# Layer 1's self-attention in a two-layer decoder: layernorms in halves, later projections, earlier first shifts, and two small copies as maxima over one element

## The chip, the cores and the metric

The kernel runs on one core of one Trainium2 chip. The metric is the device time of one execution in microseconds (us), taken as the median of several runs; lower is better.

A core has a matrix engine (TensorE, PE in the profile; its weight loads are the row PEld), a vector engine (VectorE, DVE), an activation engine (ScalarE, ACT), a general engine (GpSimd, POOL) and a queue engine that issues DMAs (SyncE, SP). Matmuls write to PSUM, of which this kernel uses three banks for short products (the tile `bank`), two double banks (the tile `wide`) and one bank for sums (the tile `acc`) in the stage that is changed.

## The reference

The whole computation is two post-layernorm decoder layers over x of shape (2, 1024, 256) in fp32. What is changed here is the fourth of six blocks, layer 1's self-attention:

```python
def _L1_attn_ref(x, W_qkv, b_qkv, W_proj, b_proj):
    B, N, C = x.shape                      # 2, 1024, 256
    qkv = x @ W_qkv + b_qkv
    qkv = qkv.reshape(B, N, 3, 16, 16).transpose(2, 0, 3, 1, 4)
    q, k, v = qkv
    scores = einsum('bhqd,bhkd->bhqk', q, k) * 16 ** -0.5
    attn = softmax(scores)
    out = einsum('bhqk,bhkd->bhqd', attn, v)
    return out.transpose(0, 2, 1, 3).reshape(B, N, C) @ W_proj + b_proj
...
x = _layernorm(x + _L0_ffn_ref(x, ...))    # its end lies in the changed stage
x = _layernorm(x + _L1_attn_ref(x, ...))
x = _layernorm(x + _L1_xattn_ref(x, ctx_1024, ...))
```

## The kernel before

The 2048 tokens are four groups g of 512 tokens (two for each batch b), held as tiles of 128 tokens: `x[g]` is 128 x 4 x 256. The stage lies in `l1_attn`.

**Units and steps.** A step is one batch b, one quad of four heads and one half qb of the queries, so there are 16 steps in the order of `steps`. A step has eight units, one for each block `kt` of 128 keys, 128 units in all. A unit computes the scores of its keys against 512 queries for four heads (`products`, L1270), adds a shift to them by a second matmul (L1276), takes the exponential on ScalarE (L1282), and one unit later multiplies the result with the values (`mix`, L1296). The shift is the row maximum of the scores, negated; it has to be known before a step begins. So every unit also computes two pieces of the scores of a step ahead (`maxima`, L1225, 18 pieces in front) and VectorE reduces each half of them (L1235), out of the three banks.

**The shifts.** At the last unit of a step, `shifts(n)` takes the smaller of two halves (L1245), rounds it to the matmul format (a copy, L1247), copies that into the tile `cz` (L1248) and writes the rest beside it by a subtraction (L1249), all on VectorE and all on 128 x 16 elements. `shifted(n)` turns `cz` on TensorE (L1256), and VectorE evacuates it.

**The other work.** Everything else is laid out by hand in a table: `at(unit, f, ...)` puts a call at the end of a unit. TensorE, VectorE and ScalarE run in the order in which their instructions are written (`manual_schedule`); instructions of GpSimd and DMAs from SP are ordered by a planner and start when what they need is there. The calls are:
- `project` computes 512 columns of q or k for eight heads (L1134), ScalarE adds the bias (L1139), VectorE cuts it to its high part (L1142), GpSimd subtracts (L1143): a split. `stacks` copies the parts by DMA into the layout of the score matmuls (32 DMAs for two steps), and `values` computes the values of two blocks of keys.
- `taken` and `quotient` divide a finished step by its row sums.
- For each finished group: `turned` transposes the result, `output` multiplies with the output weights and adds x plus the bias (a residual sum on GpSimd, L1342), then takes the moments (L175, L176, L178 on VectorE, a power on GpSimd, L180); `normed` scales (L228), and `onward` transposes x for the next block.
- The same `weigh` (moments) and `normed` end the block before for groups 2 and 3, at units 11 to 13 and 19 to 21.

With `first = 8 * n` for step n, projections stand at `first - 26`, stacks at `first - 20`, values at `first - 22`. The first group that is finished here has `first` 48, the next 56, the third 112; the fourth is finished in the next block, through the list `ends`.

Ahead of unit 0 there are nine units that only compute maxima, out of the double banks (L1230), beside the first values and projections, and after them the first shifts.

The moments are written tile by tile:

```python
for k, i in enumerate(tiles):
    nc.vector.bn_stats(st, r[:, i, :])
    nc.vector.bn_aggr(mv[:, k, :], st)
nc.vector.tensor_scalar(ve[:, 0:n], mv[:, 0:n, 1], EPS, None, ALU.add)
nc.gpsimd.tensor_tensor(rstd[:, 0:n], ve[:, 0:n], self.nhalf[:, 0:n], ALU.pow)
```

A second helper, `weighed`, is there already for another block: it does two tiles at a call, both `bn_stats` before both `bn_aggr`, and the power at the second call. `scaled_half` scales two tiles.

Of the kernel before, what the change touches and what calls it, by code (L numbers as in the profile page):

```python
# [9 lines left out]
F32 = mybir.dt.float32  # L10
# [5 lines left out]
ALU = mybir.AluOpType  # L16
AX = mybir.AxisListType

P = 128
B, S, D = 2, 1024, 256  # L20
# [13 lines left out]
class Decoder:  # L34
# [1110 lines left out]
    def l1_attn(self):  # L1145
        nc, t = self.nc, self.t
        w, parts = self.l1w, self.l1parts
        wo = self.weight(t["L1_attn_W_proj"].rearrange("(c p) o -> p c o", p=P), 2, D)
        with ExitStack() as s:
# [5 lines left out]
            for k in range(2):  # L1155
                f = self.weight(None, 1, P)[:, 0, :]
# [10 lines left out]
            def project(b, m, name, blk):  # L1167
                self.l1_project(b, m, name, blk, self.xT[2 * b + blk])
# [41 lines left out]
            def maxima(u, early=False):  # L1210

                if u >= 16 * len(steps):
                    return
                n, k = u // 16, u % 16 // 8
                qt, kb = divmod(u % 8, 2)
                b, quad, qb = steps[n]
                jp = 2 * quad + k
                if u % 16 == 0:
                    most[n] = self.sm.tile([P, 2, 4, 4], F32, tag="most", name="most")
                q0 = qb * 512 + qt * P  # L1220
                both = self.wide() if early else None
                sc = [both[:, a, :] if early else self.bank() for a in range(2)]
                for a in range(2):
                    rows = slice(64 * a, 64 * a + 64)
                    nc.tensor.matmul(  # L1225
                        sc[a], lhsT=stack[b, jp, "q"][rows, q0 : q0 + P],
                        rhs=stack[b, jp, "k"][rows, kb * 512 : (kb + 1) * 512], start=True, stop=True,
                    )
                if early:
                    nc.vector.tensor_reduce(  # L1230
                        most[n][:, kb, qt, k : k + 3 : 2], both, AX.X, ALU.max, negate=True
                    )
                for a in range(0 if early else 2):
                    h = 2 * a + k
                    nc.vector.tensor_reduce(  # L1235
                        most[n][:, kb, qt, h : h + 1], sc[a], AX.X, ALU.max, negate=True
                    )

            def shifts(n):

                if n >= len(steps):
                    return
                cz = zeros[n % 2]
                nm = self.sm.tile([P, 4, 4], F32, tag="nm8", name="nm8")
                nc.vector.tensor_tensor(nm, most[n][:, 0], most[n][:, 1], ALU.min)  # L1245
                hi = self.sm.tile([P, 4, 4], F32R, tag="nmh", name="nmh")
                nc.vector.tensor_copy(hi, nm)  # L1247
                nc.vector.tensor_copy(cz[:, :, :, 0], hi.bitcast(F32))  # L1248
                nc.vector.tensor_tensor(cz[:, :, :, 1], nm, hi.bitcast(F32), ALU.subtract)  # L1249

            def shifted(n):
# [74 lines left out]
            aT, nxT = {}, [None] * NG  # L1326

            def turned(g):
                a_tok = tok[g // 2, g % 2]
                aT[g] = self.weight(None, 2, GT)  # L1330
                for c in range(2):
                    ps = self.bank()
                    for i in range(4):
                        nc.tensor.transpose(
                            ps[:, i * P : (i + 1) * P],
                            a_tok[:, i, 2 * c : 2 * c + 2, :].rearrange("p a i -> p (a i)"), self.ident,
                        )
                    self.evac(aT[g][:, c, :], ps)

            def output(g):  # L1340
                r = self.rp.tile([P, 4, D], F32, tag="r", name="r")
                nc.gpsimd.tensor_tensor(  # L1342
                    r, self.x[g], self.lbp.unsqueeze(1).to_broadcast([P, 4, D]), ALU.add
                )
                for i in range(0, 4, 2):
                    ps = self.bank().rearrange("p (i d) -> p i d", i=2)
                    for k in range(2):
                        for c in range(2):
                            nc.tensor.matmul(
                                ps[:, k, :], lhsT=aT[g][:, c, (i + k) * P : (i + k + 1) * P],  # L1350
                                rhs=wo[:, c, :], start=c == 0, stop=c == 1,
                            )
                    rv = r[:, i : i + 2, :]
                    nc.vector.tensor_tensor(rv, ps, rv, ALU.add)
                weigh(g, r)

            sums = {}

            def weigh(g, r=None):
                r = self.sums[g] if r is None else r  # L1360
                sums[g] = r, self.moments(r, range(4))

            def normed(g):
                r, moments = sums.pop(g)
                self.x[g] = self.xp.tile([P, 4, D], F32, tag="x", name="xg")
                self.scaled(self.x[g], r, range(4), *moments)

            def onward(g):
                nxT[g] = self.transposed(self.x[g])
# [4 lines left out]
            def at(unit, f, *args):  # L1374
                extra.setdefault(unit, []).append((f, args))

            for g, unit in ((2, 11), (3, 19)):
                for k, f in enumerate((weigh, normed, self.turned)):
                    at(unit + k, f, g)
            last = 8 * len(steps)  # L1380
            both = [(name, blk) for name in "qk" for blk in range(2)]
            for n, (b, quad, qb) in enumerate(steps):
                first = 8 * n
                if qb == 0:
                    for i, (name, blk) in enumerate(both):
                        if quad % 2 == 0 and n > 4:
                            at(first - 26 + i, project, b, quad // 2, name, blk)
                    for i, name in enumerate("qk" if n else ()):
                        for k in range(2):
                            at(first - 20 + 2 * k + i, stacks, b, 2 * quad + k, name)  # L1390
                    if quad == 0 and n:
                        for k in range(4):
                            at(first - 22 + k, values, b, k)
                at(first + 8, taken, n)
                at(first + 9, quotient, n)
                if quad == 3 and n < len(steps) - 1:
                    g = 2 * b + qb
                    for k, f in ((10, turned), (11, output), (13, normed), (15, onward)):
                        at(first + k, f, g)

            def others(unit):
                for f, args in extra.pop(unit, ()):
                    f(*args)

            engines = {mybir.EngineType.PE, mybir.EngineType.DVE, mybir.EngineType.Activation}
            with self.tc.manual_schedule(engines=engines):
                for k in range(2):
                    for name in "kq":
                        stacks(0, k, name)
                jobs = [lambda k=k: values(0, k) for k in range(4)]  # L1410
                jobs += [lambda a=a: project(0, 1, *a) for a in both]
                for unit in range(-9, 0):
                    maxima(2 * unit + 18, True)
                    maxima(2 * unit + 19, True)
                    if jobs:
                        jobs.pop(0)()
                    others(unit)
                shifts(0)
                shifted(0)
                late = None  # L1420
                for unit in range(last + 1):

                    n = (unit + 1) // 8 if unit % 8 == 7 else None
                    if n:
                        shifts(n)
                    maxima(2 * unit + 18)
                    now = products(*divmod(unit, 8)) if unit < last else None
                    maxima(2 * unit + 19)
                    if n:
                        shifted(n)  # L1430
                    if late:
                        mix(*late)
                    late = now
                    others(unit)
                for unit in sorted(extra):
                    others(unit)
            self.ends = [lambda f=f: f(3) for f in (turned, output, normed, onward)]
            self.xT = nxT


# [460 lines left out]
```

## Time and profile before

| | us |
|---|---|
| median of 3 runs | 2443.83 |
| lowest and highest of them | 2438.67, 2444.66 |
| the profiled execution: its time | 2446.0 |
| the profiled execution: its span | 2444.2 |

| engine | busy us | share of the span | instructions |
|---|---|---|---|
| TensorE, matmul | 2337.1 | 96% | 14037 |
| TensorE, weight load | 1592.3 | 65% | 14037 |
| VectorE | 1676.1 | 69% | 2920 |
| ScalarE | 1107.5 | 45% | 1726 |
| GpSimd | 913.5 | 37% | 751 |

The mean granted clock of TensorE is 0.977 of full speed. Unit 0 begins at 1784.7 us of the span and unit 127 ends near 2229.7. Matmuls are pipelined and their ends are modelled, so that TensorE looks busy where it is not at its peak: what counts is what an instruction waited for. In a row of a group, the numbers after the bar are the busy time, the mean length of one in ns, and the idle time of the engine in front of it with what ended that. In a row of waits, they are the time, how often, and the longest. In a row of the timeline there are the start, the length (of several, if x is over 1), the engine, the line, and in brackets the idle time before it and what released it.

### The profile page before, as it was taken

The numbers are of one execution on the slowest core, as the hardware profiler recorded it, in microseconds if no ns is written. First come the engines' busy times: TensorE is split into PE (matmuls) and PEld (weight loads), VectorE is DVE, ScalarE is ACT, GpSimd is POOL, SyncE is SP. The second block draws the span as 40 slices with busy tenths as digits, with TensorE's granted clock in tenths as the row PEclk, the third lists the DMA queues.
The fourth block names the chain that finished last, engine by engine and source line by source line (L and its number), as shares of the span: only waits on it lengthen the run. The fifth ranks groups of instructions, "written<-read, shape, count | busy, mean of one in ns | idle before, by whom it ended". The sixth has DMA issues, their size and how long they took to land.

```text
span 2444.2 us, 37232 instructions
## 1 busy us (share of the span) xinstructions
PE 2337.1 (96%) x14037; PEld 1592.3 (65%) x14037; DVE 1676.1 (69%) x2920; ACT 1107.5 (45%) x1726; POOL 913.5 (37%) x751
## 2 busy tenths in 40 slices
PE   7999999999998999999999999999999999999974
PEld 3445545545545668899999999999744444555742
DVE  6888888988785235555565555546789687995786
ACT  4665565565562322333233333333156454665344
POOL 4666576666565222433243342432310001002412
PEclk9999999999999999999999999999989999999996
DMA  7888788788787001001010010100212122210001
GB/s 158 171 169 165 151 171 166 143 172 165 151 171 180 1 1 42 18 22 30 10 36 29 18 47 1 48 1 1 55 20 45 25 36 34 43 28 1 1 1 35
DMA packets 275715, 168.81 MB, mean 69 GB/s; under 512 B 47584, under 2 KB 262224, under 8 KB 275536
## 3 DMA queue, kind: packets, MB, share of 16 engines
q1 hardware_dynamic: 239120, 148.07, 28.8%
q10 hardware_dynamic: 36416, 18.36, 3.7%
q8 instruction: 111, 1.82, 0.3%
q14 instruction: 68, 0.56, 0.1%
HBM read 34.23 MB, written 2.10 MB: 15 GB/s over the span
## 4 chain that ended last, share of the span: by engine, by line
PE 79%; DVE 10%; SPq 3%; issue 3%; DMA 3%; ACT 2%; POOL 1%; ACTq 0%; POOLq 0%; DVEq 0%
PE unit L965 16%; PE acc L1013 9%; PE wide L325 7%; PE bank L1013 7%; PE acc L407 6%; PE acc L1296 5%; PE bank L1225 3%; PE bank L280 3%; SPq L386 3%; DVE most L1235 2%; PE bank L705 2%; PE wide L692 2%; PE bank L425 2%; PE wide L1270 2%; PE wide L1276 2%
## 5 line engine op out<-in xcount | busy, mean ns | idle before, releaser
L340 DVE TENSOR_REDUCE nm<-wide 128x1 f32<-128x1024 f32 x256 | 300.8, 1213 | 56.1 <-PE wide L325 55.2
L1235 DVE TENSOR_REDUCE most<-bank 128x1 f32<-128x512 f32 x476 | 296.0, 682 | 24.8 <-PE bank L1225 24.0
L1282 ACT ACTIVATE w<-wide 128x1024 f32<-128x1024 f32 x256 | 248.2, 1022 | 141.9 <-PE wide L1276 131.8
L325 PE MATMUL wide<-k,q 64*128 64x512 f32 x1024 | 273.0, 627 | 17.7 <-ACT p L345 14.8
L356 POOL TENSOR_SCALAR p<-p,sums 128x1024 f32<-128x1024 f32 x128 | 143.5, 1121 | 265.8 <-DVE sums L353 265.8
L407 PE MATMUL acc<-turned,v 128*64 128x256 f32 x2048 | 236.5, 384 | 1.9 <-ACT aoT L74 1.0
L407 PEld LDWEIGHTS acc<-turned,v 128*64 128x64 f32 x2048 | 144.1, 137 | 114.3 <-issue 34.2
L954 ACT ACTIVATE mhT<-mhT,cols 128x256 f32<-128x256 f32 (+1 forms) x256 | 143.3, 607 | 144.2 <-DVE mhT L982 101.1
L345 ACT ACTIVATE p<-wide,nm 128x1024 f32<-128x1024 f32 x128 | 142.8, 1116 | 135.4 <-DVE nm L340 111.2
L370 DVE STREAM_TRANSPOSE blocks<-p 128x1024 f32<-128x1024 f32 x128 | 158.0, 1234 | 49.6 <-DMA q<-q 21.5
L863 POOL TENSOR_TENSOR hs<-hs,mhT 128x1024 f32<-128x1024 f32 x31 | 102.4, 3304 | 237.4 <-DVE hs L861 220.2
L325 PEld LDWEIGHTS wide<-k,q 64*128 64x128 f32 x1024 | 90.0, 186 | 143.3 <-issue 71.3
L965 PE MATMUL unit<-xT,w 128*128 128x256 f32 x768 | 182.0, 379 | 0.0
L1022 DVE SCALAR_TENSOR_TENSOR r<-acc,gates,r 128x128 f32<-128x128 f32 x256 | 77.7, 345 | 138.1 <-PE acc L1013 138.1
L180 POOL TENSOR_TENSOR rstd<-ve,nhalf 128x4 f32<-128x4 f32 (+2 forms) x24 | 22.0, 918 | 383.5 <-DVE ve L178 383.2
L370 DVE STREAM_TRANSPOSE blocks<-r 128x1024 f32<-128x1024 f32 x128 | 153.8, 1202 | 0.0
L1225 PE MATMUL bank<-kst,qst 64*128 64x512 f32 x476 | 139.2, 480 | 14.1 <-DVE most L1235 13.8
L965 PEld LDWEIGHTS unit<-xT,w 128*128 128x128 f32 x768 | 141.0, 190 | 17.1 <-issue 0.5
L1225 PEld LDWEIGHTS bank<-kst,qst 64*128 64x128 f32 x476 | 67.7, 189 | 127.7 <-DVE most L1235 105.2
L356 POOL TENSOR_SCALAR r<-r,sums 128x1024 f32<-128x1024 f32 x128 | 143.8, 1123 | 0.0
L345 ACT ACTIVATE r<-wide,nm 128x1024 f32<-128x1024 f32 x128 | 142.2, 1111 | 1.1 <-DVE nm L340 0.9
L1296 PE MATMUL acc<-w,v 128*32 128x512 f32 x1024 | 141.6, 626 | 0.0
(341 smaller groups left out, 4592.1 us busy)
## 6 DMA issues: line engine op xcount, KB each, us to landing
turned<-blocks SPq DMA_DIRECT2D x636, 128.0 KB, 2.8
turned<-blocks ACTq DMA_DIRECT2D x132, 128.0 KB, 3.0
w<-in_L_ffn_W SPq DMA_DIRECT2D x16, 1024.0 KB, 5.7
q<-q SPq DMA_DIRECT2D x64, 128.0 KB, 2.3
k<-k SPq DMA_DIRECT2D x32, 128.0 KB, 2.4
qst<-qh SPq DMA_DIRECT2D x48, 64.0 KB
qst<-ql SPq DMA_DIRECT2D x48, 64.0 KB, 2.4
kst<-kh SPq DMA_DIRECT2D x48, 64.0 KB
```

What stands on the lines that cost most here:

```text
L325: nc.tensor.matmul(sc[h][:, kb, :], lhsT=q[rows, qi, at : at + P], rhs=k[rows, ki, :], start=True, stop=True,)
L340: nc.vector.tensor_reduce(nm, sc, AX.XY, ALU.max, negate=True)
L345: nc.scalar.activation(p, sc.rearrange("p a c -> p (a c)"), AF.Exp, bias=nm, accum_out=sums[:, 0, h : h + 1],)
L356: nc.gpsimd.tensor_scalar(p, p, sums[:, 1, h : h + 1], 1.0, ALU.mult, ALU.mult)
L370: nc.vector.transpose(blocks[m][:, :, h, qt, :], p.rearrange("p (j q) -> p j q", q=32))
L407: nc.tensor.matmul(av[own[h], 0:256].rearrange("p (t i q) -> p i t q", t=2, i=4), lhsT=vals[u][:, kt, own[h]], rhs=p[:, h], start=kt == 0, ...
L965: nc.tensor.matmul(v[:, m, :], lhsT=up[e][k][:, f : f + P], rhs=self.halves[g][k], start=k in (1, 2, 5) and m == 0, stop=True, skip_group_ ...
L1013: nc.tensor.matmul(ps[at][:, m * P : (m + 1) * P], lhsT=h[k][:, c, m * P : (m + 1) * P], rhs=down[e][k][:, c, :], start=k in (1, 2, 5) and ...
L1225: nc.tensor.matmul(sc[a], lhsT=stack[b, jp, "q"][rows, q0 : q0 + P], rhs=stack[b, jp, "k"][rows, kb * 512 : (kb + 1) * 512], start=True, s ...
L1235: nc.vector.tensor_reduce(most[n][:, kb, qt, h : h + 1], sc[a], AX.X, ALU.max, negate=True)
L1282: nc.scalar.activation(slot[:, k, :], ps[k].rearrange("p a q -> p (a q)"), AF.Exp, scale=0.25)
L1296: nc.tensor.matmul(mixed[n][o : o + 32, :], lhsT=vals[b][:, kt, 17 * h : 17 * h + 32], rhs=pT[:, a, :], start=kt == 0, stop=kt == 7, tile_ ...
```

## The change

- A layernorm comes in pieces of two tiles: `weigh` and `normed` take a half, and each half has a unit of its own. The output is also split into halves, and the residual sum has a function of its own, `residual`. With groups 2 and 3 of the block before, moments go to units 11, 12 and 19, 20, scaling to 13, 14 and 21, 22, the turn to 15 and 23. For the groups that finish here, the output goes to `first` + 11 and 12, the moments to 13 and 14, the scaling to 15 and 16, the turn onward to 17. `weighed` and `scaled_half` take the place of `moments` and `scaled`.
- Projections, stacks and values stand three units later: `first - 23`, `first - 17`, `first - 19`.
- The first shifts are written ahead of the last two maxima of the nine early units.
- The two small copies of the shifts (L1247, L1248) become maxima over an axis of one element, which give the same values.

```diff
@@ shifts @@
-                nc.vector.tensor_copy(hi, nm)
-                nc.vector.tensor_copy(cz[:, :, :, 0], hi.bitcast(F32))
+
+                nc.vector.tensor_reduce(hi, nm.unsqueeze(3), AX.X, ALU.max)
+                nc.vector.tensor_reduce(
+                    cz[:, :, :, 0], hi.bitcast(F32).unsqueeze(3), AX.X, ALU.max
+                )
                 nc.vector.tensor_tensor(cz[:, :, :, 1], nm, hi.bitcast(F32), ALU.subtract)
@@ output, weigh, normed @@
-            def output(g):
-                r = self.rp.tile([P, 4, D], F32, tag="r", name="r")
+            def residual(g):
+                r = sums[g] = self.rp.tile([P, 4, D], F32, tag="r", name="r")
                 nc.gpsimd.tensor_tensor(
                     r, self.x[g], self.lbp.unsqueeze(1).to_broadcast([P, 4, D]), ALU.add
                 )
...
+            def output(g, half):
+                ps = self.bank().rearrange("p (i d) -> p i d", i=2)
...
+                rv = sums[g][:, 2 * half : 2 * half + 2, :]
+                nc.vector.tensor_tensor(rv, ps, rv, ALU.add)
...
-            def weigh(g, r=None):
-                r = self.sums[g] if r is None else r
-                sums[g] = r, self.moments(r, range(4))
+            def weigh(g, half):
+                if half == 0:
+                    sums.setdefault(g, self.sums[g])
+                moments[g] = self.weighed(sums[g], moments.get(g))
-            def normed(g):
...
+            def normed(g, half):
+                if half == 0:
+                    new[g] = self.xp.tile([P, 4, D], F32, tag="x", name="xg")
+                self.scaled_half(new[g], sums[g], half, *moments[g])
...
@@ the table of units @@
             for g, unit in ((2, 11), (3, 19)):
-                for k, f in enumerate((weigh, normed, self.turned)):
-                    at(unit + k, f, g)
+                for k, f in enumerate((weigh, normed)):
+                    for half in range(2):
+                        at(unit + 2 * k + half, f, g, half)
+                at(unit + 4, self.turned, g)
...
-                            at(first - 26 + i, project, b, quad // 2, name, blk)
+                            at(first - 23 + i, project, b, quad // 2, name, blk)
...
-                            at(first - 20 + 2 * k + i, stacks, b, 2 * quad + k, name)
+                            at(first - 17 + 2 * k + i, stacks, b, 2 * quad + k, name)
...
-                            at(first - 22 + k, values, b, k)
+                            at(first - 19 + k, values, b, k)
...
-                    for k, f in ((10, turned), (11, output), (13, normed), (15, onward)):
-                        at(first + k, f, g)
+                    at(first + 10, residual, g)
+                    at(first + 10, turned, g)
+                    for k, f in ((11, output), (13, weigh), (15, normed)):
+                        for half in range(2):
+                            at(first + k + half, f, g, half)
+                    at(first + 17, onward, g)
@@ the nine early units @@
                 for unit in range(-9, 0):
+                    if unit == -1:
+                        shifts(0)
                     maxima(2 * unit + 18, True)
...
-                shifts(0)
                 shifted(0)
@@ the last group @@
-            self.ends = [lambda f=f: f(3) for f in (turned, output, normed, onward)]
+            both = lambda f: [f(3, half) for half in range(2)]
+            self.ends = [
+                lambda: (residual(3), turned(3)), lambda: (both(output), both(weigh)),
+                lambda: both(normed), lambda: onward(3),
+            ]
```

More of the change, by code (lines that the diff above doesn't have):

```diff
@@ L1338, in turned @@
                     self.evac(aT[g][:, c, :], ps)
-            def output(g):
-                r = self.rp.tile([P, 4, D], F32, tag="r", name="r")
+            sums = {}
+            def residual(g):
+                r = sums[g] = self.rp.tile([P, 4, D], F32, tag="r", name="r")
                 nc.gpsimd.tensor_tensor(
@@ L1344, in output @@
                 )
[L1345 to L1357, printed above, removed]
-            def weigh(g, r=None):
-                r = self.sums[g] if r is None else r
-                sums[g] = r, self.moments(r, range(4))
-            def normed(g):
-                r, moments = sums.pop(g)
-                self.x[g] = self.xp.tile([P, 4, D], F32, tag="x", name="xg")
-                self.scaled(self.x[g], r, range(4), *moments)
+            def output(g, half):
+                ps = self.bank().rearrange("p (i d) -> p i d", i=2)
+                for k in range(2):
+                    for c in range(2):
+                        i = 2 * half + k
+                        nc.tensor.matmul(
+                            ps[:, k, :], lhsT=aT[g][:, c, i * P : (i + 1) * P],
+                            rhs=wo[:, c, :], start=c == 0, stop=c == 1,
+                        )
+                rv = sums[g][:, 2 * half : 2 * half + 2, :]
+                nc.vector.tensor_tensor(rv, ps, rv, ALU.add)
+            moments = {}
+            def weigh(g, half):
[6 more added lines that the diff above has]
+                self.scaled_half(new[g], sums[g], half, *moments[g])
+                if half:
+                    self.x[g] = new.pop(g)
+                    del sums[g], moments[g]
+            new = {}
             def onward(g):
```

## The prediction

> **What bounds the kernel now.** I read the page first, then the waits of the stretch from 1784 to 2232 us (layer 1's self-attention), then the timeline there, and last the windows, which give each stretch's own work. The page's groups show what the stage runs on:
>
> ```profile
> span 2444.2 us, 37232 instructions
> L1235 DVE TENSOR_REDUCE most<-bank 128x1 f32<-128x512 f32 x476 | 296.0, 682 | 24.8 <-PE bank L1225 24.0
> L1225 PEld LDWEIGHTS bank<-kst,qst 64*128 64x128 f32 x476 | 67.7, 189 | 127.7 <-DVE most L1235 105.2
> ```
>
> The reader is to see a ring: VectorE's maxima are fed by three PSUM banks, and TensorE waits 105 us for a maximum to give a bank back. The waits of the stage alone say how often (in us, times, longest):
>
> ```profile
> PEld bank L1225 <- DVE most L1235: 105.2, 129, 2.6
> ```
>
> So the stage is priced unit by unit, a unit running from its first score matmul (L1270) to the next unit's. The windows below are, in order, a plain unit, one with a projection (38), the step change with a projection (39), the unit after it (40), one with values (44), a plain step change (47), the unit with a whole layernorm's moments (60), and step change 71. The columns are length, busy time of PE, PEld, DVE, ACT, POOL, then the granted clock.
>
> ```profile
> 1880.96:1883.67 2.71, 2.71 (x23) 1.39 (x20) 2.48 (x4) 1.94 (x2) 0.00 (x0) 1.00 0.00 0
> 1907.24:1911.86 4.62, 4.62 (x26) 2.06 (x24) 2.48 (x4) 2.10 (x3) 0.00 (x0) 1.00 0.21 34
> 1911.86:1922.41 10.55, 8.70 (x31) 3.42 (x28) 4.97 (x10) 2.63 (x4) 1.29 (x1) 0.68 0.00 0
> 1922.41:1927.72 5.31, 4.99 (x26) 2.06 (x24) 2.82 (x5) 3.21 (x5) 1.28 (x1) 1.00 0.00 2
> 1943.60:1948.46 4.86, 4.86 (x31) 2.82 (x28) 3.14 (x7) 1.94 (x2) 0.00 (x0) 1.00 0.00 0
> 1956.26:1960.12 3.86, 3.74 (x28) 1.80 (x25) 3.59 (x9) 1.94 (x2) 0.00 (x0) 1.00 0.43 68
> 2000.33:2006.95 6.62, 4.50 (x22) 1.73 (x20) 5.00 (x14) 1.94 (x2) 1.02 (x1) 0.75 0.00 0
> 2050.69:2060.68 9.99, 8.04 (x38) 3.92 (x36) 5.56 (x11) 3.21 (x5) 1.28 (x1) 0.83 0.00 0
> ```
>
> A plain unit is 2.70 us, of which VectorE works 2.48: it has 0.22 us of slack, and anything longer that it does between two units lengthens the unit. A step change is 3.85, a projection 1.92 in its unit and 0.68 in the next, values 2.16. Units 39, 60 and 71 are longer than their parts. The timeline around unit 39 says why:
>
> ```profile
> 1912.97 1.29 POOL L1143 TENSOR_TENSOR ql<-w,qh 128x512 f32<-128x512 f32 x1 [54.52 <-DVE nm L1245]
> 1913.17 1.13 DVE L1248 COPY cz<-nmh 128x16 f32<-128x16 f32 x1
> 1915.03 0.79 PE L1225 MATMUL bank<-kst,qst 64*128 64x512 f32 x1 [1.85 <-DVE most L1235]
> 1916.79 1.94 PE L1296 MATMUL acc<-w,v 128*32 128x512 f32 x8
> ```
>
> The small copy of the shifts normally takes 0.183 us; here it ends with POOL's split of the projection. TensorE starves 1.85 us, and then its mix takes 1.94 instead of 1.07: the clock has halved. The clock changes on a grid of 3.41 us; windows laid on that grid, just ahead of three drops and one without a drop, show the condition:
>
> ```profile
> 1822.73:1826.14 3.41, 1.76 (x12) 0.34 (x9) 3.31 (x10) 1.71 (x2) 1.01 (x1) 1.00 0.00 0
> 1911.47:1914.89 3.42, 1.71 (x12) 1.05 (x11) 2.41 (x6) 2.63 (x3) 1.29 (x1) 1.00 0.00 0
> 2051.42:2054.83 3.41, 1.47 (x9) 0.72 (x6) 3.34 (x8) 1.94 (x2) 1.28 (x1) 1.00 0.00 0
> 2034.35:2037.77 3.42, 3.07 (x18) 2.01 (x17) 2.32 (x7) 0.93 (x2) 0.00 (x0) 1.00 0.48 77
> ```
>
> Windows with up to 1.77 us of matmul are followed by half clock; those with about 2.5 or more are not.
>
> **A rule weighed: the clock.** The Trainium skill, "TensorE: Matmul & The Clock Gate", section "Why this matters for your kernels", warns only of idle gaps over about 3 us. Here a gap of 1.65 to 1.85 us was enough. By the page, breaking a 2.4 us lump of VectorE work in two would leave the clock as it is, and the 3.7 us of units 60 to 62 and 68 to 70 below would stay; by the rows they go. I go by the rows.
>
> **The change part by part** (against the profiled execution: span 2444.2, time 2446.0, which is 2.2 above the median 2443.83).
>
> Projections three units later. Unit 39: 10.55 - 3.85 - 0.68 - 1.92 = 4.1 us too long. Unit 71: 9.99 - 3.85 - 1.92 - 0.68 - 1.1 (turning x onward, from unit 63: 4.96 - 3.85) = 2.4. At units 41 to 44 and 73 to 76 no shift lies near a split, so both go: -6.5. The projections and values themselves cost what they cost now. Their stack DMAs, 32 for each pair of steps at 0.59 us of SP issue, already start at 1835.1, 1886.8, 1956.7, 2014.7, 2086.4 and 2133.5, that is in units 15, 31, 47, 63, 79 and 95: the four buffers come free there, at exactly the unit they are moved to, and nothing else stands in SP's queue. I put 0. Only the pair for step 2 really moves, from an end at 1781.4 to about 1800, and it is needed at unit 7 (1806); without that cover it would cost those few us once.
>
> Pieces. Now a layernorm's moments are a chain of 2.42 us (1821.67 to 1824.09) and its scaling 1.37; less the slack, 2.2 and 1.15. In halves I estimate 0.95 and 1.1 for the moments (two statistics 0.33 apart, then two aggregates that no longer wait one for another), 0.65 each for the scaling; less four times 0.22, 2.5 instead of 3.35. With the turn now in step change 15 or 23, where it should cost the 1.1 of unit 63 rather than 1.25, layernorms 2 and 3 win 1.0 each: -2.0. For groups 0 and 1 the output in halves costs 2.16 twice (the values' row, also 8 matmul records and 0.7 us of VectorE) in place of 3.86; that eats the 0.6 saved on the moments. What they win is the clock: units 60 to 62 took 13.98 against 3 x 2.70 + 2.2 + 1.15 = 11.45, units 68 to 70 14.57 against 13.37 (with a projection): -3.7. Group 2's layernorm falls in units 122 to 129, which have no maxima and 2.12 us each; TensorE's sum there is unchanged: 0, within 1 us either way, since its turn now follows the last mix.
>
> Early first shifts. Now TensorE waits 3.22 us for them (1779.90 to 1783.12). Ahead of the last two wide maxima they would start at 1779.95, but POOL's last split runs 1780.14 to 1781.40. If the subtraction waits for it, the maxima end at 1783.7 instead of 1782.3, and the evacuation that releases the products starts at 1783.66 rather than 1784.25: -0.6. Unhindered -1.3, and -3 if the half clock from 1781.77 to 1792.0 goes too. I take -0.6.
>
> Maxima of one. The trace has no such reduction; nearest are its own two copies (174 and 183 ns) and long reductions whose fixed part is 150 ns (682 for 512). Between -0.3 and +0.5 us for 32; I take 0.
>
> Sum of these: -6.5 - 2.0 - 3.7 - 0.6 = -12.8.
>
> **A rule against it: the shared port.** Alone, L861 takes 1.21 us. Beside a POOL sum:
>
> ```profile
> 1059.22 1.28 POOL L872 TENSOR_TENSOR w2s<-w,w2s 128x512 f32<-128x512 f32 x1
> 1059.29 2.29 DVE L861 TENSOR_TENSOR hs<-mhT 128x1024 f32<-128x1024 f32 x1
> ```
>
> The skill's "SBUF — State Buffer", "Who interferes with whom", says a reduction never contends on this chip, but a VectorE instruction with two SBUF inputs does with a GpSimd instruction that reads SBUF. The subtraction right behind the two copies (L1249) has two SBUF inputs. So the reductions move the wait by one instruction and do not remove it. And the pieces bring new meetings. The residual sum of group 0 starts as soon as layernorm 2 gives up its buffer:
>
> ```profile
> 1826.39 1.37 DVE L228 TENSOR_SCALAR xg<-r,mv,rstd 128x256 f32<-128x256 f32 x4
> 1827.84 2.38 POOL L1342 TENSOR_TENSOR r<-xg,lbp 128x1024 f32<-128x1024 f32 x1 [2.66 <-DVE xg L228]
> ```
>
> Now only PSUM maxima follow, which don't care. After the change the last scaling stands at the end of units 14 and 22, and the shifts of steps 2 and 3 come next on VectorE: the subtraction, some 0.5 us into the 2.38, waits 1.85. Behind it queue the maxima, and for those TensorE. Two such: +3.7 (0 if the rule fails; up to 6.7 with a slow window after each). The power on POOL (1.0 us) now ends the moments just ahead of step changes 63 and 71: 0 to 0.55 each, I take +0.5 in all, as four elements may not hold the port throughout. The residual sums of groups 2 and 3 follow the last split (2073.98 to 2078.73); three units later the second ends 7.0 us after unit 77 begins (as now after 74), and the shifts of unit 79 begin after about 6.1: 0 to 1.2, I take +0.6. By the rule +4.8, without it nothing.
>
> Forecast: -12.8 + 4.8 = -8.0 on the profiled execution (2438.0), or 2435.8 on the median; I say 2436.
>
> **The rivals.**
> A: the full gain. The subtraction, of 16 elements, slips past POOL, and the first shifts gain 1.3: about -13, 2431. For it speaks that no row shows L1249 itself waiting; against it, L861.
> B: slow windows return. The lump at 63 and 71 is still about 1.7 us (half of the moments, scaling aside, then the shifts) and 2.2 with POOL's power; 15 and 23 lose 1.85 in one stroke. If each of the four costs 1.0 more: -4, 2440. For it, windows of 1.77 already drop; against it, the drops at 1826.1 and 1853.4 cost nothing, since VectorE was the bound there.
> C, slower: the port becomes the bound of the step changes. At 15, 23 and 79 each wait (1.85) is followed by two slow windows (the 3.1 us that unit 39 lost beyond its 0.95), at 63 and 71 by 0.5 + 3.1. That is 14.9 + 7.2 = 22 against 12.8: +9, 2453. It decides from 12.8 us upwards; against it, unit 39 also held a projection's TensorE work, which those don't.
> That the copies' edit does nothing is part of the forecast.
>
> **How the numbers follow.** A difference under 0.3% (7.3 us) is about what a measurement of this kernel can't tell from none. The forecast (2433.5 to 2438.5) has 0.40, of which 0.30 is beyond that bound since its centre is; A 0.24, all faster; B 0.20, all within; C 0.16, 0.14 slower and 0.02 within. Faster 0.54, same 0.32, slower 0.14. The range runs from 2428 (A with the starting clock saved too) to 2447, and leaves C out. The likely side, faster, alone would be 2428 to 2436.5.
>
> **What would show it.** Right: units 39 and 71 near 5; no copy or small reduction over 0.2 us; L1249 over 1.5 us at units 15 and 23 beside L1342's sum; half-clock windows after 2000 gone. Wrong: L1249 at 0.18 everywhere (A), half clock after 63 and 71 (B), step changes of 8 us or more at 15, 23, 79 (C), or stack DMAs that start after units 15, 31, 47.

## The result, and the profile after

The changed kernel takes 2433.13 us (median of 19 runs, 2428.12 to 2441.28) against 2442.77 us (19 runs, 2436.23 to 2448.59) of the kernel before, run beside it. The ratio is 0.9964, with a 95% interval from 0.9953 to 0.9975: 9.6 us less where 8.0 was forecast, and inside the range of the prediction. Of the 2.9 us by which it lies below the forecast of 2436, 1.1 come from the kernel before, which measures 2442.77 here and not 2443.83.

The page and the waits of the stage (1784 to 2220 us) after the change:

```profile
span 2431.3 us, 37229 instructions
L1235 DVE TENSOR_REDUCE most<-bank 128x1 f32<-128x512 f32 x476 | 295.2, 681 | 19.4 <-PE bank L1225 18.8
L1225 PEld LDWEIGHTS bank<-kst,qst 64*128 64x128 f32 x476 | 67.1, 186 | 125.8 <-DVE most L1235 104.1
```
```profile
PEld bank L1225 <- DVE most L1235: 104.1, 139, 2.9
```

The ring of maxima and banks is the same, and it still sets the pace; TensorE's wait in it has hardly moved. What moved is seen in single units. Behind the shifts, lines of the changed kernel stand higher: the subtraction is L1252, the residual sum L1347, the two maxima of one L1248 and L1249. The windows are units 39, 60, 71, 15 and 23, and step change 79, with the columns as in the prediction:

```profile
1908.75:1912.60 3.85, 3.74 (x26) 1.80 (x24) 3.59 (x9) 1.94 (x2) 0.00 (x0) 1.00 0.03 5
1993.41:1998.21 4.80, 4.80 (x30) 2.82 (x28) 3.08 (x6) 1.94 (x2) 0.00 (x0) 1.00 0.00 0
2036.32:2041.11 4.79, 3.73 (x27) 1.81 (x24) 4.69 (x15) 1.94 (x2) 1.01 (x1) 1.00 0.00 0
1827.68:1836.55 8.87, 6.34 (x34) 3.48 (x32) 6.71 (x12) 2.27 (x3) 2.36 (x1) 0.81 0.54 87
1857.88:1865.25 7.37, 4.85 (x34) 2.55 (x31) 6.70 (x12) 2.25 (x3) 2.36 (x1) 1.00 0.00 0
2072.39:2077.02 4.63, 3.73 (x27) 1.80 (x25) 4.37 (x9) 1.94 (x2) 0.93 (x1) 1.00 0.45 72
```

Units 39 and 71, 10.55 and 9.99 us before, are now step changes at full clock. Units 15 and 23 were 3.74 and 3.75 before; 15 has more than doubled and 23 nearly so, though all that was moved into them is the turn and the end of the last scaling. (Below, a meeting is a GpSimd instruction that runs beside the shifts, and a slow window is a stretch at half clock.) The timeline of unit 15 shows what they wait for:

```profile
1827.59 0.72 DVE L228 TENSOR_SCALAR xg<-r,mv,rstd 128x256 f32<-128x256 f32 x2
1828.23 0.16 DVE L1245 TENSOR_TENSOR nm<-most 128x16 f32<-128x16 f32 x1
1828.39 2.36 POOL L1347 TENSOR_TENSOR r<-xg,lbp 128x1024 f32<-128x1024 f32 x1 [5.05 <-DVE nm L1245]
1828.43 0.17 DVE L1248 TENSOR_REDUCE nmh<-nm 128x16 fp32r<-128x16 f32 x1
1828.63 0.18 DVE L1249 TENSOR_REDUCE cz<-nmh 128x16 f32<-128x16 f32 x1
1828.72 2.07 DVE L1252 TENSOR_TENSOR cz<-nm,nmh 128x16 f32<-128x16 f32 x1
1830.70 2.47 DVE L1235 TENSOR_REDUCE most<-bank 128x1 f32<-128x512 f32 x4
1831.44 0.50 PE L1225 MATMUL bank<-kst,qst 64*128 64x512 f32 x1 [2.44 <-DVE most L1235]
```

The last scaling of layernorm 2 ends, GpSimd starts the residual sum of group 0, the two maxima of one pass beside it at 0.17 and 0.18 us, and the subtraction ends where the sum ends. TensorE starves for 2.44 us behind it.

**The balance of one profiled execution.** The two executions reach the stage at different times: the first memset of the values starts at 1753.80 before and at 1750.31 after, although nothing ahead of it was changed. So the stage is measured from that memset, and to the first score matmul of unit 127: 472.88 us before, 463.80 after, 9.08 less. By parts, from the starts of units in the two timelines (negative is shorter):

| part | predicted | measured |
|---|---|---|
| memset to unit 2 (first shifts) | -0.6 | -0.33 |
| units 10 to 24 (layernorms 2 and 3, the residual sums' meetings) | +1.7 | +2.64 |
| units 38 to 49 (first projections) | -4.1 | -3.95 |
| units 58 to 79 (groups 0 and 1, second projections, unit 79) | -5.0 | -7.60 |
| units 122 to 126 (group 2) | 0 | +0.21 |
| sum | -8.0 | -9.03 |

The sum comes out near the forecast partly by luck: one part is 0.9 us worse and another 2.6 us better than was priced.

### The profile page after: what moved, and what is told of

Read it like the earlier page. It is cut to its first block, busy times and chain, and to the rows that moved or that the text cites. A ratio compares the mean times of both kernels' runs of the same rounds, so it can differ in the third digit from the quotient of the medians.

```text
span 2431.3 us, 37229 instructions
## 1 busy us (share of the span) xinstructions
PE 2324.3 (96%) x14034; PEld 1586.7 (65%) x14037; DVE 1675.2 (69%) x2920; ACT 1106.9 (46%) x1726; POOL 912.9 (38%) x751
## 4 chain that ended last, share of the span: by engine, by line
PE 75%; DVE 12%; DMA 3%; issue 3%; SPq 3%; ACT 2%; POOL 1%; ACTq 0%; POOLq 0%; DVEq 0%
PE unit L965 16%; PE acc L1013 9%; PE bank L1013 7%; PE wide L325 6%; PE acc L407 5%; PE acc L1299 4%; PE bank L280 3%; PE bank L1225 3%; DVE most L1235 3%; SPq L386 3%; PE bank L705 2%; PE wide L692 2%; DMA turned<-blocks 2%; PE bank L425 2%; DVE nm L340 2%
## 5 line engine op out<-in xcount | busy, mean ns | idle before, releaser
L390 POOL COPY turned<-blocks 32x1024 f32<-32x1024 f32 x128 | 131.8, 1029 | 4.0 <-DVE blocks L370 0.3
```

## The experiments

All kernels ran beside the kernel before on their chip; ratios are against it. "From the memset" is always the stretch from the first memset of the values to unit 127.

**Copies back.** The changed kernel, with

```diff
-                nc.vector.tensor_reduce(hi, nm.unsqueeze(3), AX.X, ALU.max)
-                nc.vector.tensor_reduce(
-                    cz[:, :, :, 0], hi.bitcast(F32).unsqueeze(3), AX.X, ALU.max
-                )
+                nc.vector.tensor_copy(hi, nm)
+                nc.vector.tensor_copy(cz[:, :, :, 0], hi.bitcast(F32))
```

> The changed kernel with its two maxima over one element turned back into copies. Theory 1 (the shared port; whichever of the small instructions comes first with a need for it waits, so the maxima only move the wait): the same time within 0.1% of the changed kernel; units 15 and 23 as now (8.9 and 7.4 us), with the wait of about 2 us on a copy instead of on the subtraction; the first shifts wait 0.7 us on a copy as they do now on the subtraction. Theory 2 (the maxima free the step changes, and a good part of the 9.6 us gained is theirs): 2 to 4 us slower, with waits at step changes 15, 23, 63, 71 that are longer than now by about 1 us each. At 63 and 71 theory 1 leaves open whether a copy waits for the power on GpSimd, since the subtraction did not.

Measured: 2436.07 us (14 runs), ratio 0.9975 [0.9964, 0.9987]. Its timeline at unit 15:

```profile
1830.33 2.35 POOL L1344 TENSOR_TENSOR r<-xg,lbp 128x1024 f32<-128x1024 f32 x1 [5.06 <-DVE nm L1245]
1830.37 2.35 DVE L1247 CAST nmh<-nm 128x16 fp32r<-128x16 f32 x1
1832.75 0.18 DVE L1248 COPY cz<-nmh 128x16 f32<-128x16 f32 x1
1832.83 0.18 DVE L1249 TENSOR_TENSOR cz<-nm,nmh 128x16 f32<-128x16 f32 x1
```

The wait stands on the first copy, and the subtraction behind it is free again: theory 1 as to place. As to time it is 2.9 us slower than the changed kernel on the medians, 0.12%, though the two intervals overlap; 0.1% was expected, and theory 2's number is near. The profile says where: from the memset 466.53, 2.7 longer. Unit 15 took 9.17 (against 8.87) and unit 23 9.18 (against 7.37). At 63 and 71 nothing waited (4.82 and 4.81), so two of theory 2's four places are wrong. The copy starts 0.28 us earlier into the sum than the subtraction does, VectorE starves TensorE that much longer, and here a half-clock window followed in both units; in the changed kernel only in unit 15.

**Layernorms 2 and 3 one unit earlier.** The changed kernel, with

```diff
-            for g, unit in ((2, 11), (3, 19)):
+            for g, unit in ((2, 10), (3, 18)):
```

> The changed kernel with all of the work of layernorms 2 and 3 one unit earlier (moments at units 10, 11 and 18, 19, scaling at 12, 13 and 20, 21, turn at 14 and 22), so that the residual sums on GpSimd run beside maxima and not beside the shifts. Theory 1 (the residual sum holds the port against the subtraction): the subtraction falls from 2.07 to 0.18 us at units 15 and 23, units 10 to 16 and 18 to 24 lose 3.9 and 2.4 us in sum, and the execution is 5 to 6.5 us shorter than the changed kernel. Rival (units 15 and 23 are long because the turn, the shifts and the stack DMAs stand in one unit; the wait of the subtraction is hidden by TensorE's work): the gain is what the turn costs elsewhere, under 1 us, and unit 14 grows by as much as 15 shrinks.

Measured: 2428.71 us (6 runs), ratio 0.9943 [0.9928, 0.9959]; from the memset 457.58, 6.2 shorter than the changed kernel. Its units 14 and 15:

```profile
1826.33:1830.48 4.15, 4.15 (x31) 2.13 (x27) 3.77 (x8) 2.25 (x3) 2.38 (x1) 1.00 0.01 4
1830.48:1834.17 3.69, 3.59 (x26) 1.93 (x27) 3.44 (x9) 2.21 (x3) 0.00 (x0) 1.00 0.34 53
```

```profile
1826.87 2.48 DVE L1235 TENSOR_REDUCE most<-bank 128x1 f32<-128x512 f32 x4
1827.04 2.38 POOL L1347 TENSOR_TENSOR r<-xg,lbp 128x1024 f32<-128x1024 f32 x1 [5.06 <-DVE xg L228]
1830.83 0.18 DVE L1252 TENSOR_TENSOR cz<-nm,nmh 128x16 f32<-128x16 f32 x1
```

The residual sum now lies beside maxima from PSUM, which it does not slow (four of them take 2.48 us, as in a plain unit), and the subtraction takes 0.18 us. Units 14 and 15 take 7.84 us together where they took 11.90. The rival falls.

**Projections alone.** The kernel before, with

```diff
-                            at(first - 26 + i, project, b, quad // 2, name, blk)
+                            at(first - 23 + i, project, b, quad // 2, name, blk)
...
-                            at(first - 20 + 2 * k + i, stacks, b, 2 * quad + k, name)
+                            at(first - 17 + 2 * k + i, stacks, b, 2 * quad + k, name)
...
-                            at(first - 22 + k, values, b, k)
+                            at(first - 19 + k, values, b, k)
```

> The kernel before with only the projections, stacks and values three units later. Theory 1 (a split on GpSimd met the copy of the shifts at units 39 and 71, and the starved window halved the clock): units 38 to 49 lose 4.0 us, unit 71 loses its wait and slow window, 2.4 us, and the half-clock windows at 1914.9 and 2054.8 go; the copies are 0.18 us at all step changes but perhaps 79, where the residual sum now ends into the shifts; 5 to 6.5 us faster than before. Rival (units 39 and 71 were long since a projection's TensorE work and a step change stood in one unit, and the copy's wait lay beside it): under 1.5 us faster, the TensorE work turns up in the units it moves to.

Measured: 2437.42 us (22 runs), ratio 0.9978 [0.9970, 0.9986], 5.0 us faster on the medians; from the memset 468.47, 4.4 shorter. Its units 39, 71 and 79:

```profile
1907.93:1911.80 3.87, 3.74 (x27) 1.82 (x24) 3.60 (x9) 1.94 (x2) 0.00 (x0) 1.00 0.02 3
2043.33:2048.29 4.96, 4.86 (x35) 2.56 (x31) 4.29 (x10) 2.26 (x3) 0.00 (x0) 1.00 0.00 0
2078.24:2082.86 4.62, 3.73 (x28) 1.81 (x25) 4.35 (x9) 1.94 (x2) 0.92 (x1) 1.00 0.44 71
```

Units 38 to 49 lost 3.92 us, and units 39 and 71 are free of wait and slow clock; unit 79 gained 0.77, with the minimum (L1245) taking 0.94 us in place of 0.17 beside the residual sum, as expected. The TensorE work did turn up where it was moved, but the wait and the slow window did not: the rival falls. In this execution the moments of group 1 were followed by two half-clock windows and not one (unit 68 took 1.3 us more), which hides most of the gain of unit 71. With group 0 it was the other way round: two such windows before, one here. So the same starved stretch cost one window in one execution and two in another.

**Pieces alone.** The kernel before with halves of layernorms and outputs (`weigh`, `normed`, `output`, `residual` and their units as in the change), and the rest as before.

> The kernel before with only the pieces: layernorms and output in halves; projections, first shifts and copies as before. Theory 1: units 11 to 16 and 19 to 24 are 2.7 us longer in sum (now the copy waits for the residual sum), units 58 to 70 lose about 5 us, among them the slow windows at 2003.6 and 2041.2, unit 39 stays at 10.5; unit 71 keeps a copy's wait of 1 us for the split. In sum 1 to 4 us faster than before. Rival (the pieces carry most of the 9.6 us): 6 us or more faster. Other rival (pieces cost more in split outputs than they give back): slower than before.

Measured: 2439.22 us (14 runs), ratio 0.9992 [0.9980, 1.0003]; from the memset 469.69, 3.2 shorter. Its units 15, 39 and 71:

```profile
1818.98:1828.22 9.24, 6.41 (x34) 3.14 (x31) 7.00 (x12) 2.25 (x3) 2.36 (x1) 0.82 0.52 85
1904.43:1913.67 9.24, 7.29 (x30) 2.98 (x28) 4.88 (x10) 2.62 (x4) 1.29 (x1) 0.82 0.00 0
2034.74:2043.93 9.19, 7.24 (x30) 2.84 (x28) 5.53 (x12) 2.63 (x4) 1.52 (x2) 0.81 0.00 0
```

Units 10 to 24 are 5.1 us longer (2.7 was expected; each of the two meetings drew a slow window), units 58 to 65 are 3.8 shorter, units 39 and 71 stay long. So the pieces alone can't be told from the kernel before: most of what they give groups 0 and 1 they lose at 15 and 23. The profile is of the fastest of the 14 executions (2430.6 us), so the 3.2 us from the memset is not the gain of a usual one.

**No subtraction.** The changed kernel without the line of the subtraction, which leaves the low part out of every shift.

> The changed kernel without the subtraction of the shifts (it leaves out the low part of every shift; the column stays zero). The residual sums still start beside the shifts of units 15 and 23. Theory 1 (only the subtraction waits for the port, the maxima of one do not): the waits of 2.07 us vanish with nothing moved, units 15 and 23 fall to 5.0 or less, the first shifts no longer wait, the minimum at unit 79 still waits 0.95; 6 to 7 us shorter than the changed kernel from the stage's first memset to unit 127. Rival (the residual sum slows anything that VectorE does there): a reduction or the first maxima take the wait over and units 15 and 23 stay over 7 us.

Measured: 2428.57 us (4 runs), ratio 0.9938 [0.9917, 0.9960]; from the memset 456.41, 7.4 shorter than the changed kernel. At unit 15:

```profile
1828.88 2.37 POOL L1346 TENSOR_TENSOR r<-xg,lbp 128x1024 f32<-128x1024 f32 x1 [5.05 <-DVE nm L1245]
1828.92 0.17 DVE L1248 TENSOR_REDUCE nmh<-nm 128x16 fp32r<-128x16 f32 x1
1829.12 0.18 DVE L1249 TENSOR_REDUCE cz<-nmh 128x16 f32<-128x16 f32 x1
1829.21 2.47 DVE L1235 TENSOR_REDUCE most<-bank 128x1 f32<-128x512 f32 x4
```

The sum is where it was, and nothing waits. Units 15 and 23 (5.0 was expected):

```profile
1828.17:1833.57 5.40, 4.85 (x35) 2.55 (x31) 4.73 (x11) 2.26 (x3) 2.37 (x1) 1.00 0.45 73
1855.11:1860.50 5.39, 4.84 (x34) 2.55 (x31) 4.73 (x11) 2.25 (x3) 2.37 (x1) 1.00 0.00 0
```

That settles it: of the instructions that stand there it is the subtraction alone that waits.

**Early first shifts alone.** The kernel before, with `shifts(0)` ahead of the last two wide maxima.

> The kernel before with only the first shifts ahead of the last two wide maxima, with copies. Theory 1 (they meet the last split on GpSimd): a copy waits about 1.2 us until the split ends; from the memset of the values to unit 2 it is 0 to 0.5 us shorter than before (38.9), the rest of the stage is unchanged, so within 0.1% of before. Rival (the wait of 3.2 us on TensorE goes as a whole, and the half clock with it): 2 us or more shorter to unit 2.

Measured: 2439.88 us (20 runs), ratio 0.9988 [0.9979, 0.9997]. To unit 2 it takes 38.73 us from the memset against 38.87.

```profile
1775.45 1.26 POOL L1143 TENSOR_TENSOR kl<-w,kh 128x512 f32<-128x512 f32 x1 [1.72 <-DVE nm L1245]
1775.49 1.25 DVE L1247 CAST nmh<-nm 128x16 fp32r<-128x16 f32 x1
```

A copy waits until the last split ends (1.25 us in place of 0.17), and of the 3.2 us that TensorE waited almost nothing is won. Where the rest of the 2.65 us on the medians comes from is not shown; in the profiled execution unit 39 (1.6 us) and units 58 to 65 (1.3 us), which this edit does not touch, lost less to slow windows than in that of the kernel before.

**All meetings taken away, two tries.** The changed kernel with layernorms 2 and 3 one unit earlier, projections, stacks and values one unit earlier (`first - 24`, `- 18`, `- 20`), and in the early units all projections ahead of the values; once with maxima of one, once with copies.

> The changed kernel with every meeting of the shifts with GpSimd taken away by order alone: layernorms 2 and 3 one unit earlier, projections, stacks and values one unit earlier (first - 24, - 18, - 20), and in the nine early units the projections ahead of the values. Theory 1: no small instruction of the shifts over 0.2 us anywhere; against the changed kernel 5.9 us from the layernorms (as in the run with them alone), 0.8 at unit 79, 0.7 or, where the half clock at the start shortens, up to 3 at the first shifts: 7 to 9 us shorter, about 2425. Rival (the clock at the start and the table load rule the start, and the stack DMAs of step 12 come too late or too early): no better than the run with earlier layernorms alone, 2428.7.

> The same kernel as the one with every meeting taken away, but with copies in place of the maxima of one. Theory 1 (where nothing on GpSimd runs beside the shifts, it is one whether they are copies or maxima): the same time within 0.1%, except that the power at step changes 63 and 71 might hold a copy; the run with the copies back showed no wait there, so I expect none. Rival (the maxima have a worth of their own): 1 us or more slower, seen at every step change, of which there are 16.

Measured: 2432.64 us (6 runs), ratio 0.9949 [0.9930, 0.9967], and with copies 2431.27 us (6 runs), 0.9947 [0.9928, 0.9967]. The first misses the 2425 that was expected of it; the second is within 0.1% of the first, as expected. None of the small instructions waits in either, and units 0 to 127 take 428.13 and 428.34 us (434.60 in the changed kernel), so copies and maxima are worth the same once nothing runs beside them. But from the memset to unit 2 they take 43.43 and 44.05 us, over 4 more than any other kernel here. The timeline of the first of them shows where:

```profile
1759.11 1.26 ACT L1139 ACTIVATE w<-bank,cols 128x512 f32<-128x512 f32 x2 [18.51 <-DMA qst<-xg]
```

The projections' biases are ScalarE's work, and ScalarE stands behind the stack DMAs that it issues itself; the values' bias is VectorE's work (L1187), and in the old order the values covered that time.

**Two moves, and the last values.** The same without the new order in the early units; and then with only the last `values` put behind the projections.

> The changed kernel with layernorms 2 and 3 one unit earlier and projections, stacks and values one unit earlier, but the nine early units in their old order (the run that put all projections first lost 5 us there, as ScalarE, behind its stack DMAs, first added a bias 18 us late). Theory 1: to unit 2 as in the changed kernel (38.3 to 38.5 from the memset of the values), 15 and 23 near 3.7, unit 79 at 3.85: 7 us shorter than the changed kernel, about 2427. Rival: what is won at 79 is lost by the projection that now directly follows step change 39: as the run with earlier layernorms alone, 2428.7, or slower.

> The same, and in the nine early units only the last values are moved behind the projections, so that the last split ends 3 us earlier and the first shifts meet nothing. Theory 1: the first subtraction falls from 0.89 to 0.18 us and the memset to unit 2 takes 0.7 us less than in the changed kernel (up to 2 where the half clock at the start is shorter); otherwise as the run without it: about 2426. Rival (ScalarE or a buffer holds the projections, as in the run that put them first): 1 us or more longer to unit 2.

Measured: 2426.65 us (6 runs), ratio 0.9934 [0.9914, 0.9954]; and 2426.98 us (6 runs), 0.9934 [0.9916, 0.9952]; about 2427 and 2426 were expected. The first, at units 15 and 79:

```profile
1830.51:1834.20 3.69, 3.59 (x26) 1.94 (x27) 3.44 (x9) 2.21 (x3) 0.00 (x0) 1.00 0.33 53
2067.29:2071.13 3.84, 3.72 (x27) 1.80 (x24) 3.58 (x9) 1.94 (x2) 0.00 (x0) 1.00 0.39 62
```

From the memset they take 456.81 and 455.38 us, 7.0 and 8.4 less than the changed kernel. The second one's subtraction is at most 0.18 us everywhere, and to unit 2 it needs 37.10 us against 38.76; in the times the two can't be told apart. Either beats both kernels: about 6.5 us below the changed one and 15 below the one before.

## Why the prediction was right

- **Projections.** "At units 41 to 44 and 73 to 76 no shift lies near a split, so both go": shown by the run with the projections alone. Of the 4.1 us at units 38 to 49, 3.92 to 3.95 came.
- **The stack DMAs.** They still start in units 15, 31, 47, 63, 79 and 95, and no unit that needs them grew, as predicted at 0.
- **The residual sum against the subtraction.** "The subtraction, some 0.5 us into the 2.38, waits 1.85": it took 2.07 in place of 0.18, so 1.89. That it is the subtraction and the sum is shown from two sides, by moving the sum and by leaving the subtraction out. The rule that the prediction took from the Trainium skill ("SBUF — State Buffer", "Who interferes with whom") held in both halves beside the sum: a reduction passes at 0.17 us, an instruction with two SBUF inputs waits. (Beside the power, below, its second half did not hold.) So rival A is out.
- **Unit 79.** The second residual sum "ends 7.0 us after unit 77 begins" and the shifts begin "after about 6.1": it came out as 7.03 and 6.11. The prediction carried 0.6; the minimum, which also has two SBUF inputs, took 0.96 in place of 0.17 and the unit grew by 0.77.
- **The clock.** The rows were the better guide: with the lumps cut in two, no slow window began in units 58 to 70, here or in the run with the pieces alone. On the grid of this execution, the window of 3.41 us ahead of the drop in unit 15, and the one at unit 63, which no drop followed:

```profile
1829.54:1832.95 3.41, 1.42 (x9) 0.76 (x13) 3.41 (x5) 0.81 (x1) 1.21 (x1) 1.00 0.60 100
2003.62:2007.03 3.41, 2.47 (x19) 1.26 (x12) 3.31 (x13) 2.03 (x3) 1.02 (x1) 1.00 0.23 37
```

Rival B had one of its four slow windows, in unit 15 but not at 23, 63 or 71. Rival C is out on the time; of its signs, step changes of 8 us or more at 15, 23 and 79, only unit 15 shows one (8.87, against 7.37 and 4.63).

Four terms were mis-sized, and partly cancel.

- **The pieces won more for groups 0 and 1 than was counted.** Units 58 to 78 did 2.8 us better than forecast, 0.5 of it by the next term. For the rest, two steps of the sum fall short. It counted for these groups the clock alone, although the prediction's own prices leave a gain: scaling falls from 1.15 to 0.86 in halves, and the split output takes 0.46 of the 0.6 saved on the moments. That is 0.4 for each group. And "less four times 0.22" took off too little. Behind a piece VectorE waits for no bank (in unit 12, below, it is busy throughout), and each instruction starts before the one ahead of it has ended: in units 12 to 14 it is 2.37 to 2.40 us from the first of four maxima to what follows them, and not 2.48, so that the slack of a 2.70 us unit is 0.3. The pieces themselves, 0.88, 1.06 and twice 0.64 us, were 0.13 shorter than estimated. By these figures, as an estimate, 0.9 us of the 1.1 for each group are explained.

```profile
1817.95:1821.18 3.23, 3.07 (x22) 1.38 (x20) 3.23 (x9) 1.94 (x2) 0.00 (x0) 1.00 0.00 0
```

- **The power on GpSimd did not hold up the subtraction.** Predicted +0.5. At step change 63 the subtraction, with two SBUF inputs, ran beside it at its usual length, and so it did at 71 (0.17):

```profile
2005.46 1.02 POOL L199 TENSOR_TENSOR rstd<-ve,nhalf 128x4 f32<-128x4 f32 x1 [66.90 <-DVE nm L1245]
2005.78 0.17 DVE L1252 TENSOR_TENSOR cz<-nm,nmh 128x16 f32<-128x16 f32 x1
```

- **A slow window followed one of the two meetings.** The run without the subtraction is the measure: there units 15 and 23, with the turn and the sum but no wait, take 5.39, and a plain step change 3.76 in place of 3.85, so that the subtraction's own work is 0.09. Counted with the unit behind it (10.28 against 8.31 us), and less that 0.09, unit 23's meeting cost 1.9 us, its wait as priced; unit 15's cost 3.2 (11.57 against 8.30). The 1.3 between them is the slow window, which the prediction had in its range and not in its sum; it is more than the 0.9 by which units 10 to 24 did worse than forecast. The layernorm and its turn were priced right in sum: without a wait, units 11 to 16 take 3.5 us more than plain units and a step change would, against 2.5 + 1.1.
- **The first shifts were worth 0.33 rather than 0.6.** The subtraction took 0.89 us, up to the end of the split, and the half clock at the start stayed; both were in the sum. Where the other 0.27 went is open.

Not settled is the exact condition for the drop. In the middle of the stage, over all twelve traces, full-clock windows with up to 1.77 us of matmul were followed by one, and those from 1.94 up were not; at the start of the stage a window of 2.46 us was (in the run with the last values moved). That window holds transposes and matmuls that wait for the first shifts; what of it counts for the clock no run here tells.

## What to carry to other kernels

When a small VectorE instruction is now and then ten times as long, look at what GpSimd runs in that moment, and go through all of the instructions that stand in a row there: here, replacing the copies that waited only handed the wait to the subtraction behind them. Moving the GpSimd work by one place in the order was worth more than changing the instructions (6.2 us from the memset against 2.7, and nothing where nothing ran beside them). And when work is cut into pieces, ask what its last piece releases, and what will then stand beside that.

## What the runs showed of the hardware that was not expected

- A power of four elements on GpSimd takes 1.02 us but leaves a subtraction with two SBUF inputs alone (0.17 us), while a sum of 1024 elements holds it until its end (2.07). So the length of an instruction on GpSimd does not by itself say how long VectorE waits beside it.
- The copy to the matmul format that started 0.04 us after GpSimd's sum waited for all of it (2.35 us); in the kernel before, one that started 0.01 us before the split took its 0.17.
- The same kernel's executions differ by 13 us (2428.12 to 2441.28). With one profile for each kernel, the reason is not shown. A likely part is the slow windows: across the kernels' profiles, the same starved stretch was followed by one of them or two, about 1.3 us apart.
